# Graph attention, layer 1: the turn of two sets' gathered rows, as 16 row tiles of 64 keys in one place instead of 8 full transposes in two

## The chip, the cores and the metric

The kernel runs on one core of a Trainium2 chip. Its time is device microseconds (us) of one execution. TensorE is called PE in the profile (PEld is its weight load), VectorE is DVE, ScalarE is ACT, GpSimd is POOL, SyncE is SP.

## The reference

A two-layer graph attention over 2048 nodes in 8 batches with a residual and two layer norms. All data is float32; `adj` is a 0/1 matrix that all batches and heads share.

```python
def _gat_layer(h, mask, b):
    scores = jnp.einsum('...nd,...md->...nm', h, h)
    scores = jnp.where(mask, scores, NEG)
    attn = jax.nn.softmax(scores, axis=-1)
    return jnp.einsum('...nm,...md->...nd', attn, h) + b

mask = graph + jnp.eye(N, dtype=graph.dtype) > 0            # N = 2048
h = jnp.einsum('bnc,hdc->bhnd', x, Wh)                      # 8 batches, 4 heads, 64 wide
out_h = _gat_layer(h, mask[None, None], bh[None, :, None, :])        # layer 1
z = jax.nn.leaky_relu(cat, negative_slope=0.2)              # cat: the heads side by side
h2 = jnp.einsum('bnk,dk->bnd', z, Wo)
out2 = _gat_layer(h2, mask[None], bo)                       # layer 2
...                                                         # leaky, norm, residual, norm
```

## The kernel before

The graph is sparse except for 56 hub nodes, which are done densely. The other 1992 nodes stand in 166 sets of 12. For each set the kernel finds a list of at most 128 keys (the neighbours of any of its nodes), gathers the 128 rows of these keys from a table in device memory (an indirect DMA of POOL, L829), and does the attention of the set's nodes against them. One gathered row holds a node in all 8 batches: four pairs of batches (`q`), each of 130 numbers, of which 128 are the 64 channels of two batches (`p`), between two columns of ones.

Layer 1 is a loop over 83 groups of two sets. The order of the work is the order in which the loop is written; each engine runs its own instructions in that order and waits on counts of the others. The loop is a software pipeline: step i works at several groups at once. On TensorE one step does, in this order:

- `scores` of group i+1 (L858): the turned rows as weights, 64x64 tiles of the array, four at a time;
- `project` of group i-1 (L551), 64x64 tiles, from the tile `otb` that ACT copies in `keep_values` (L907) out of the turned values;
- `values` of group i (L883): the exponentials `e` as weights, 128x64 tiles, two at a time;
- `second_maps` of group i-2 (L917), 128x64 tiles, and `second_rows` of group i-3 (L927, a transpose), both into the tile `cat`;
- `columns` for group i+4 (L843, full 128x128), also into `cat`: the products from which the scores' moving side `y` is made;
- `turn(bank[0], ...)`: four transposes of 128x128 (L532), the rows of the first set of group i+3 into one PSUM bank;
- `turn_values` of group i (L900): four transposes of the weighted values `osb` that DVE has divided (L890, L891);
- `turn(bank[1], ...)`: four more transposes, the rows of the second set.

A float32 matmul stands in the trace as two records of its form, a transpose as one.

The other engines in a step: ACT adds the bias to `project`'s result (`z`, L538, two instructions), then copies the two banks with the turned rows of group i+2 to the tile `xTg` in SBUF (L1182, two copies), raises `e` to its exponential (L870), copies the columns (`keep_columns`, `y<-cat`, L849) and the turned values (`keep_values`, `otb<-o`, L907). DVE subtracts the mask from the scores (`weigh`, L863), divides the values (L890, L891), does the leaky maximum of `z` (L543), copies the second maps out of `cat` (`keep_own`, `own<-cat`, L922), adds the bias to the second rows (`keep_rows`, `rowt<-cat`, L931), and then does one or two jobs of the search for the key lists, while there are any. The banks `bank[0]` and `bank[1]` are single: what turns rows into them has to wait until ACT has copied the rows of the group before.

Of the kernel before, what the change touches and what calls it, by code (L numbers as in the profile page):

```python
# [359 lines left out]
def fast_kernel(ctx: ExitStack, tc: tile.TileContext, x, adj, Wh, bh, Wo, bo, gamma, beta, out, flag):  # L360


    nc = tc.nc
    B, N, C = x.shape
    H, D, _ = Wh.shape
    P = 128
    NB = N // P
    Q = B // 2
# [6 lines left out]
    NG = NS // 2  # L375
    M = SET * H
# [23 lines left out]
    def half(k):  # L400
        return slice(k * 64, (k + 1) * 64)

    def rows_tile(name):
        return rowp.tile([P, Q, PW], F32, tag="rows", name=name)
# [7 lines left out]
    ident = const.tile([P, P], F32, name="ident")  # L412
# [116 lines left out]
    def turn(tp, rows):  # L529

        for q in range(Q):
            nc.tensor.transpose(tp[:, q * P:(q + 1) * P], rows[:, q, 1:1 + P], ident)  # L532

    def leaky(cat, n, name):

        z = work.tile([P, HP, 2, n], F32, tag="z", name=name, bufs=3)
        for hp in range(HP):
            nc.scalar.activation(z[:, hp], cat[:, :, hp * n:(hp + 1) * n], AF.Identity, bias=bhp[:, hp:hp + 1], scale=1.0)  # L538
        return z

    def leak(z):
        f = z.rearrange("p q s n -> p (q s n)")
        nc.vector.scalar_tensor_tensor(f, f, SLOPE, f, OP.mult, OP.max)  # L543

    def project(ot, cat, n):

        for hp in range(HP):
            for s in range(2):
                for j in range(2):
                    h = 2 * hp + j  # L550
                    nc.tensor.matmul(cat[half(j), s, hp * n:(hp + 1) * n], whT[half(s), h * D:(h + 1) * D],  # L551
                                     ot[half(s), h, :], start=True, stop=True)
# [268 lines left out]
    rows = {}  # L821
    held = {}
# [9 lines left out]
    def own_rows(m):  # L832
# [3 lines left out]
        src = xT[:, :, HUB:].rearrange("c q (k s) -> c s q k", s=NS)[:, 4 * m:4 * m + w]  # L836
        nc.gpsimd.tensor_copy(t[:, :w * 48].rearrange("c (s q k) -> c s q k", s=w, q=Q), src)

    def columns(g, cat):

        n = min(4, NS - 4 * (g // 2)) * 48
        for k in range(2):
            nc.tensor.matmul(cat[:, k, 2 * GM:2 * GM + n], gram[:, g % 2 * 2 + k, :], held["x", g // 2][:, :n], start=True, stop=True)  # L843
# [5 lines left out]
        nc.scalar.copy(held["y", g // 2][:, :n, g % 2 * 2:g % 2 * 2 + 2], cat[:, :, 2 * GM:2 * GM + n].rearrange("p a n -> p n a"))  # L849

    def scores(g, sp):
        xt = held.pop(("T", 1, g)).rearrange("c j (q n) -> c j q n", q=Q)
        y = held["y", g // 2][:, g % 2 * GM:(g % 2 + 1) * GM, :].rearrange("p n h -> p (n h)")
        for j in range(2):
            for q in range(Q):
                for p in range(2):
                    for r in range(2):
                        nc.tensor.matmul(sp[half(r), p, (q * 2 + j) * M:(q * 2 + j + 1) * M], xt[half(p), j, q, half(r)],  # L858
                                         y[half(p), (j * Q + q) * M:(j * Q + q + 1) * M], start=True, stop=True)

    def weigh(g, sp):
        e = es[g % 2]
        nc.vector.tensor_tensor(e[:, :16 * M].rearrange("p (a q n) -> p a q n", a=2, q=Q),  # L863
                                sp[:, :, :8 * M].rearrange("p a (q n) -> p a q n", q=Q),
                                mask[:, 2 * g:2 * g + 2, :].rearrange("p s n -> p (s n)").unsqueeze(1).unsqueeze(1)
                                .to_broadcast([P, 2, Q, 2 * M]), OP.subtract)

    def lift(g):
        e = es[g % 2]
        nc.scalar.activation(e[:, :16 * M], e[:, :16 * M], AF.Exp, bias=shifts[:, 0:1], scale=1.0)  # L870
# [3 lines left out]
    def values(g, op):  # L874
        e = es[g % 2]
        rw = [rows.pop((1, 2 * g + j)) for j in range(2)]
        for q in range(Q):
            for j in range(2):
                for p in range(2):
                    c0 = (p * 8 + q * 2 + j) * M  # L880
                    o0 = q // 2 * OQ + q % 2 * (D + 2) + p

                    nc.tensor.matmul(op[half(p), j, o0:o0 + K1], e[:, c0:c0 + 64], rw[j][:, q, sums(p)], start=True, stop=True)  # L883

    def invert(g, op):
        v = op.rearrange("a j (k c) -> a (j k) c", k=2)[:, :, :2 * (D + 2)].rearrange("a w (s c) -> a w s c", s=2)
        osb = held["o", g] = work.tile([P, 4, 2, D], F32, tag="osb", name=f"osb{g}")
        r = rall[:, g, :].rearrange("a (w s) -> a w s", w=4)
        for p in range(2):
            nc.vector.reciprocal(r[half(p)], v[half(p), :, :, p * K1])  # L890
        nc.vector.tensor_tensor(osb, v[:, :, :, 1:K1], r.unsqueeze(3).to_broadcast([P, 4, 2, D]), OP.mult)  # L891
# [34 lines left out]
    def second_rows(g, pr):  # L926
        nc.tensor.transpose(pr, held.pop(("own", g)), ident)  # L927
# [135 lines left out]
    bank = [psumk.tile([P, 512], F32, name=f"bank{k}") for k in range(2)]  # L1063
# [3 lines left out]
    def one(name, tag):  # L1067
        return psum1.tile([P, 2, 512], F32, tag=tag, name=name)
# [94 lines left out]
    for i in range(-3, NG + 3):  # L1163
        if 0 <= i + 1 < NG:
            sp = one(f"s{i + 1}", "S")
            scores(i + 1, sp)
            weigh(i + 1, sp)
        if i >= 1 and slow and len(slow) % 3:
            slow.pop(0)()
        cat = one(f"cat{i}", "C") if i <= NG else None  # L1170
        if i < NG:
            ph, pr = cat[:, 0, 384:384 + GM], cat[:GM, 1, 384:512]
        else:
            cat = one(f"cat{i}", "S" if i == NG + 1 else "C")
            ph, pr = cat[:, 0, :GM], cat[:GM, 1, :P]
        if 0 <= i - 1 < NG:
            project(held.pop(("ot", i - 1)), cat, GM)
            held["z", i - 1] = leaky(cat, GM, f"z{i - 1}")
        if 0 <= i + 2 < NG:
            t = held["T", 1, i + 2] = work.tile([P, 2, 512], F32, tag="xTg", name=f"xTg{i + 2}", bufs=3)  # L1180
            for k in range(2):
                nc.scalar.copy(t[:, k, :], bank[k])  # L1182
        if 0 <= i + 1 < NG:
            lift(i + 1)
        if 0 <= i < NG:
            op = one(f"o{i}", "O")
            values(i, op)
            invert(i, op)
        if 0 <= i + LOOK < NG and i > -3:
            for j in range(2):  # L1190
                gather(table1, 2 * (i + LOOK) + j, 1, rows_tile)
        if NG - LOOK <= i < NG - 1:
            for j in range(2):
                k = 2 * (i - NG + LOOK) + j
                hub_block(k, rows_tile(f"gh{k}"))
        if i + 6 < NG and i % 2 == 0 and i >= -2:
            own_rows((i + 6) // 2)
        if i >= 60 and i % 2 == 0 and ahead_of_second:
            ahead_of_second.pop(0)()
        if 0 <= (i - 30) // 2 <= NV:  # L1200
            (add_beta if i % 2 else load_own)((i - 30) // 2)
        if 0 <= i - 1 < NG:
            leak(held["z", i - 1])
        if i >= 0:
            if turns():
                some(1)
            if slow and len(slow) % 3 == 0:
                slow.pop(0)()
            more(1)
            if todo3 and i == todo3[0][0]:  # L1210
                r = todo3.pop(0)[1:]
                make_keys(*r, late_two)
                if r == (1, 1):
                    picks += pick(1)
                    done = 2 * FIRST
            if not picks:
                ready = done
            if not picks and not todo3 and done < NS:
                picks = pick(2)
                done = NS  # L1220
            assert i + 1 + LOOK >= NG or 2 * (i + 1 + LOOK) + 1 < ready

        if 0 <= i - 2 < NG:
            second_maps(i - 2, ph)
        if 0 <= i - 3 < NG:
            second_rows(i - 3, pr)
        if 2 <= i + 4 < NG + NG % 2:
            columns(i + 4, cat)
        if 0 <= i - 2 < NG:
            keep_own(i - 2, ph)  # L1230
        if 0 <= i - 3 < NG:
            keep_rows(i - 3, pr)
        for _ in range((2 if i < 22 or i % 2 else 1) if i >= 0 else 0):
            if not turns():
                some(1)
        if 2 <= i + 4 < NG + NG % 2:
            keep_columns(i + 4, cat)
        if 0 <= i + 3 < NG:
            turn(bank[0], rows[1, 2 * (i + 3)])
        if 0 <= i < NG:  # L1240
            turn_values(i, op)
            keep_values(i, op)
        if 0 <= i + 3 < NG:
            turn(bank[1], rows[1, 2 * (i + 3) + 1])
        if NG - 3 <= i < NG:
            hub_step(i - NG + 3, bank[0])
    for k in range(3, 9):
# [300 lines left out]
```

## Time and profile before

| what | value |
|---|---|
| three runs | 861.07, 863.03, 866.28 us, median 863.03 |
| the profiled execution | 860.43 us, of which the core's span is 858.6 us |
| PE busy / weight load busy | 760.2 us (89%) / 651.4 us (76%) |
| DVE, ACT, POOL busy | 601.5 us (70%), 537.9 us (63%), 485.3 us (57%) |
| granted TensorE clock, mean of the span | 0.97 |
| steps of layer 1: first and last start of `values` | 136.79 us and 577.75 us (83 steps) |

A busy PE is not PE at its peak, since records of matmuls that follow each other overlap. So the time of a run of matmuls is read from where one run starts to where the next one starts, and the step from one start of `values` (L883) to the next. The stretch before 136 us makes the lists and the hubs, the stretch after 583 us is layer 2; the change leaves both alone.

### The profile page before, as it was taken

What the parts mean: (1) busy time and instruction counts of PE and PEld (TensorE: products, weight loads), DVE (VectorE), ACT (ScalarE), POOL (GpSimd) and SP (SyncE); (2) the same over time, 40 slices, a digit from 0 to 9 for tenths busy, and PEclk for the clock granted to TensorE, in tenths of its full rate; (3) what the DMA queues carried; (4) which work ended last, traced back from release to release, by engine and by line L of the source; (5) the groups of instructions that cost most, each with busy time, mean ns of one, the idle gap of its engine ahead of it and who ended that gap; (6) DMA issues with size and microseconds to landing.
All of it is one profiled execution on the core that took longest, in us unless ns stands there. A gap on an engine that the chain in (4) does not pass through costs nothing.

```text
span 858.6 us, 42821 instructions
## 1 busy us (share of the span) xinstructions
PE 760.2 (89%) x18461; PEld 651.4 (76%) x18461; DVE 601.5 (70%) x1368; ACT 537.9 (63%) x1175; POOL 485.3 (57%) x619
## 2 busy tenths in 40 slices
PE   4798788899999999999999999998999899998940
PEld 3575567788888898988998988887887778876730
DVE  4347974688887788886556665564248999997895
ACT  2354545566666666666666666663558889887741
POOL 5444563564454456655665666504777777777700
PEclk9899989999999999999999999999999999999975
DMA  6999652443333344444444444335975666665621
GB/s 124 214 243 268 192 171 53 111 118 89 92 88 89 83 118 134 129 120 129 128 130 120 123 123 117 90 108 146 310 202 170 181 189 193 191 180 166 185 55 34
DMA packets 81791, 122.53 MB, mean 143 GB/s; under 512 B 35568, under 2 KB 51852, under 8 KB 81594
## 3 DMA queue, kind: packets, MB, share of 16 engines
q0 software_dynamic: 26784, 65.84, 28.7%
q1 hardware_dynamic: 50374, 52.71, 21.5%
q8 instruction: 148, 2.42, 1.2%
q10 hardware_dynamic: 4436, 1.15, 0.7%
q14 instruction: 49, 0.40, 0.2%
HBM read 123.91 MB, written 18.48 MB: 166 GB/s over the span
## 4 chain that ended last, share of the span: by engine, by line
PE 61%; DVE 17%; DMA 9%; issue 5%; SPq 3%; ACT 3%; POOL 2%; DVEq 0%; POOLq 0%; ACTq 0%
PE o L883 10%; PE s L858 9%; PE bank L532 8%; PE cat L843 6%; DMA rows<-table,index 5%; PE cat L551 4%; PE o L900 3%; PE cat L917 3%; PE t L532 3%; SPq L1400 3%; PE oh L639 3%; PE cat L927 2%; PE sh L621 2%; DMA out_dram<-y_s 2%; PE o L1317 2%
## 5 line engine op out<-in xcount | busy, mean ns | idle before, releaser
L829 POOL DMA_INDIRECT g<-table,index x166 | 175.6, 1058 | 173.6 <-PE o L883 144.8
L829 POOL DMA_INDIRECT rows<-table,index x166 | 173.7, 1046 | 55.1 <-issue 23.2
L863 DVE TENSOR_TENSOR e<-s,mask 128x768 f32<-128x768 f32 x83 | 79.3, 955 | 73.5 <-PE s L858 70.3
L538 ACT ACTIVATE z<-cat,bhp 128x192 f32<-128x192 f32 x166 | 60.7, 416 | 79.4 <-PE cat L551 79.3
L532 PE MATMUL t<-ident,rows 128*128 128x128 f32 x664 | 93.0, 279 | 11.2 <-DMA rows<-table,index 5.2
L883 PE MATMUL o<-g,e 128*64 128x65 f32 x2656 | 97.9, 225 | 3.9 <-issue 3.8
L532 PE MATMUL bank<-ident,g 128*128 128x128 f32 x664 | 99.5, 273 | 1.4 <-DVE e L1059 1.2
L883 PEld LDWEIGHTS o<-g,e 128*64 128x64 f32 x2656 | 85.4, 138 | 14.6 <-issue 4.8
L858 PEld LDWEIGHTS s<-y,xTg 64*64 64x64 f32 x5312 | 85.2, 135 | 13.8 <-issue 13.8
L858 PE MATMUL s<-y,xTg 64*64 64x48 f32 x5312 | 95.5, 221 | 0.0
L1436 ACT COPY xts<-t 128x512 f32<-128x512 f32 x166 | 88.7, 583 | 8.6 <-PE t L532 7.7
L532 PEld LDWEIGHTS t<-ident,rows 128*128 128x128 f32 x664 | 72.9, 141 | 24.0 <-issue 12.2
L1182 ACT COPY xTg<-bank 128x512 f32<-128x512 f32 x166 | 89.0, 596 | 2.5 <-PE bank L532 2.5
L532 PEld LDWEIGHTS bank<-ident,g 128*128 128x128 f32 x664 | 79.0, 141 | 4.1 <-issue 1.3
L849 ACT COPY y<-cat 128x384 f32<-128x384 f32 (+1 forms) x82 | 41.6, 508 | 64.1 <-PE o L900 34.5
L870 ACT ACTIVATE e<-e,shifts 128x768 f32<-128x768 f32 x83 | 80.1, 965 | 2.0 <-DVE e L863 2.0
L711 POOL TENSOR_SCALAR a<-raw 120x1024 bf16<-120x1024 int32 (+1 forms) x34 | 38.5, 1134 | 65.5 <-DMA raw<-in_adj_dram 50.6
L628 ACT ACTIVATE e<-e,shifts 128x896 f32<-128x896 f32 x32 | 33.4, 1043 | 58.1 <-DVE e L625 47.8
L890 DVE RECIPROCAL rall<-o 64x8 f32<-64x8 f32 x166 | 33.9, 205 | 47.8 <-PE o L883 46.5
L843 PE MATMUL cat<-xo,gram 128*128 128x192 f32 (+1 forms) x328 | 66.6, 326 | 0.0
L891 DVE TENSOR_TENSOR osb<-o,rall 128x512 f32<-128x512 f32 x83 | 57.4, 692 | 2.9
L625 DVE TENSOR_TENSOR e<-sh,maskh 128x896 f32<-128x896 f32 x32 | 34.8, 1087 | 31.6 <-PE sh L621 26.6
(195 smaller groups left out, 1529.8 us busy)
## 6 DMA issues: line engine op xcount, KB each, us to landing
raw<-in_adj_dram SPq DMA_DIRECT2D x32, 480.0 KB
table<-xb SPq DMA_DIRECT2D x22, 256.0 KB
xr_s<-table SPq DMA_DIRECT2D x21, 256.0 KB
table<-x SPq DMA_DIRECT2D x16, 260.0 KB
table<-rowt SPq DMA_DIRECT2D x164, 24.4 KB
xb<-in_x_dram SPq DMA_DIRECT2D x164, 24.0 KB
out_dram<-y_s SPq DMA_DIRECT2D x162, 24.0 KB
x<-in_x_dram SPq DMA_DIRECT2D x24, 128.0 KB
```

The source lines that it names most:

```text
L532: nc.tensor.transpose(tp[:, q * P:(q + 1) * P], rows[:, q, 1:1 + P], ident)
L538: nc.scalar.activation(z[:, hp], cat[:, :, hp * n:(hp + 1) * n], AF.Identity, bias=bhp[:, hp:hp + 1], scale=1.0)
L829: nc.gpsimd.indirect_dma_start(out=t.rearrange("n q c -> n (q c)"), out_offset=None, in_=table, in_offset=bass.IndirectOffsetOnAxis(ap=ind ...
L843: nc.tensor.matmul(cat[:, k, 2 * GM:2 * GM + n], gram[:, g % 2 * 2 + k, :], held["x", g // 2][:, :n], start=True, stop=True)
L849: nc.scalar.copy(held["y", g // 2][:, :n, g % 2 * 2:g % 2 * 2 + 2], cat[:, :, 2 * GM:2 * GM + n].rearrange("p a n -> p n a"))
L858: nc.tensor.matmul(sp[half(r), p, (q * 2 + j) * M:(q * 2 + j + 1) * M], xt[half(p), j, q, half(r)], y[half(p), (j * Q + q) * M:(j * Q + q ...
L863: nc.vector.tensor_tensor(e[:, :16 * M].rearrange("p (a q n) -> p a q n", a=2, q=Q), sp[:, :, :8 * M].rearrange("p a (q n) -> p a q n", q= ...
L870: nc.scalar.activation(e[:, :16 * M], e[:, :16 * M], AF.Exp, bias=shifts[:, 0:1], scale=1.0)
L883: nc.tensor.matmul(op[half(p), j, o0:o0 + K1], e[:, c0:c0 + 64], rw[j][:, q, sums(p)], start=True, stop=True)
L891: nc.vector.tensor_tensor(osb, v[:, :, :, 1:K1], r.unsqueeze(3).to_broadcast([P, 4, 2, D]), OP.mult)
L1182: nc.scalar.copy(t[:, k, :], bank[k])
L1436: nc.scalar.copy(xts[s // 2 % 4][:, s % 2, :], tp)
```

## The change

The two calls of `turn` are taken out of the loop. In their place a new function turns the rows of both sets of group i+3 in one run, between `second_rows` and `columns`. It takes each 128 keys as two halves of 64: half 0 is a transpose on the upper 64 rows of the array and goes to `bank[0]`, half 1 one on the lower 64 rows and goes to `bank[1]`. So there are 16 transposes, with 64x128 weights (the rows) and a 64x64 identity that moves, where there were 8 with 128x128 and a 128x128 identity; each bank now holds one half of the keys of both sets, and `scores` reads its weights by the new layout. `turn_values` now comes right after `columns`, and `scores` right after `turn_values`.

```diff
+    def turn_rows(g):
+
+        for j in range(2):
+            rw = rows[1, 2 * g + j]
+            for q in range(Q):
+                for r in range(2):
+                    c0 = (j * Q + q) * 64
+                    nc.tensor.transpose(bank[r][:, c0:c0 + 64], rw[half(r), q, 1:1 + P], ident[half(r), half(r)])
+
...
     def scores(g, sp):
-        xt = held.pop(("T", 1, g)).rearrange("c j (q n) -> c j q n", q=Q)
+        xt = held.pop(("T", 1, g)).rearrange("c r (j q n) -> c r j q n", j=2, q=Q)
...
-                        nc.tensor.matmul(..., xt[half(p), j, q, half(r)],
+                        nc.tensor.matmul(..., xt[half(p), r, j, q, :],
...
+        if 0 <= i + 3 < NG:
+            turn_rows(i + 3)
         if 2 <= i + 4 < NG + NG % 2:
             columns(i + 4, cat)
...
-        if 0 <= i + 3 < NG:
-            turn(bank[0], rows[1, 2 * (i + 3)])
         if 0 <= i < NG:
             turn_values(i, op)
             keep_values(i, op)
-        if 0 <= i + 3 < NG:
-            turn(bank[1], rows[1, 2 * (i + 3) + 1])
```

Lines from the new function on stand 9 further down in the changed kernel: `scores` is L867, `values` L892, `second_maps` L926, `second_rows` L936, `turn_values` L909, `keep_own` L931, `keep_rows` L940, `keep_columns` L858, `keep_values` L916, the copies of the banks L1191. The new transposes are L846, `columns` is L852. `project` and ACT's `z` keep L551 and L538.

TensorE's instructions of one step before, from `second_maps` to the next `scores`, with what they wait for in brackets (`g` is a gathered tile; the counts are those of ACT, DVE, PE itself and the gathers, DMASW):

```order
L917 MATMUL cat_3228<-z_3103,woT 64x2x4x12 x3
L927 MATMUL cat_3228<-ident,own_3167 96x128
L843 MATMUL cat_3228<-xo_2910,gram 128x192 x2
L532 MATMUL bank_1747<-ident,g_28_3017 128x128 [waits DMASW1_49,Activation_49]
L532 MATMUL bank_1747<-ident,g_28_3017 128x128 x3
L900 MATMUL o_3244<-ident,osb_3261 128x112 [waits DVE_49]
L900 MATMUL o_3244<-ident,osb_3261 128x112 x3
L532 MATMUL bank_1748<-ident,g_29_3021 128x128 [waits DMASW2_49,Activation_49]
L532 MATMUL bank_1748<-ident,g_29_3021 128x128 x3
L858 MATMUL s_3307<-y_2929,xTg_3240 64x48 [waits PE_49]
```

The bank copies of ACT are waited for at the first transpose into each bank; here `columns` stand ahead of the first of them. The same place of a step in the changed kernel (bank_1747 is `bank[0]`, bank_1748 is `bank[1]`; the transposes go on in turn where rows are left out):

```order
L926 MATMUL cat_2832<-z_2718,woT 64x2x4x12 x3
L936 MATMUL cat_2832<-ident,own_2780 96x128
L846 MATMUL bank_1747<-ident,g_20_2616 128x64 [waits DMASW1_49,Activation_49]
L846 MATMUL bank_1748<-ident,g_20_2616 128x64 [waits Activation_49]
...
L846 MATMUL bank_1747<-ident,g_21_2620 128x64 [waits DMASW2_49]
L846 MATMUL bank_1748<-ident,g_21_2620 128x64
...
L852 MATMUL cat_2832<-xo_2497,gram 128x192 x2
L909 MATMUL o_2848<-ident,osb_2865 128x112 [waits DVE_49]
L909 MATMUL o_2848<-ident,osb_2865 128x112 x3
L867 MATMUL s_2919<-y_2536,xTg_2844 64x48 [waits PE_49]
```

Both waits for ACT's copies have moved ahead of `columns`, into the first two transposes. DVE's row in a step of the changed kernel, which reads as it did before but for the line numbers:

```order
L899 RECIPROCAL rall<-o_7726 64x8 [waits PE_49]
L899 RECIPROCAL rall<-o_7726 64x8
L900 TENSOR_TENSOR osb_7743<-o_7726,rall 128x512 [waits DVE_49]
L543 SCALAR_TENSOR_TENSOR z_7719<-z_7719 128x384 [waits Activation_49]
L931 COPY own_7789<-cat_7710 128x96 [waits PE_49,Pool_49]
L940 TENSOR_TENSOR rowt_115<-cat_7710,bob 96x128 [waits DMAHW7_49,DMAHW0_49]
L872 TENSOR_TENSOR e_110<-s_7804,mask 128x768 [waits PE_49]
```

Nothing moved on DVE, but what L931 waits for did: TensorE's count is raised once for `second_maps`, `second_rows` and `columns` together, at the last matmul of `columns`, before and after; with the change that one raise covers the 16 transposes too, which stand ahead of it. ACT's row is unchanged as well:

```order
L538 ACTIVATE z_8460<-cat_8451,bhp 128x192 [waits PE_49]
L538 ACTIVATE z_8460<-cat_8451,bhp 128x192
L1191 COPY xTg_8463<-bank_1747 128x512
L1191 COPY xTg_8463<-bank_1748 128x512
L879 ACTIVATE e_111<-e_111,shifts 128x768 [waits DVE_49,Activation_49]
L858 COPY y_8536<-cat_8451 128x192x2 [waits DVE_49,PE_49]
L916 COPY otb_8542<-o_8467 128x4x48 [waits PE_49,Activation_49]
```

Here too only the source of the waits moved: L858's wait for DVE is one for `keep_rows` (both read `cat`), and `keep_values` stands behind it.

More of the change, by code (lines that the diff above doesn't have):

```diff
@@ L857, in scores @@
                     for r in range(2):
-                        nc.tensor.matmul(sp[half(r), p, (q * 2 + j) * M:(q * 2 + j + 1) * M], xt[half(p), j, q, half(r)],
+                        nc.tensor.matmul(sp[half(r), p, (q * 2 + j) * M:(q * 2 + j + 1) * M], xt[half(p), r, j, q, :],
                                          y[half(p), (j * Q + q) * M:(j * Q + q + 1) * M], start=True, stop=True)
```

## The prediction

> **What bounds the kernel now.** I read the chain that ended last first, then the engines' shares by stage, then one quiet step of layer 1 engine by engine. The chain (shares of the span) and the waits of TensorE inside layer 1 (engine, line, what ended the wait: us in total, times, longest):
>
> ```profile
> PE 61%; DVE 17%; DMA 9%; issue 5%; SPq 3%; ACT 3%; POOL 2%; DVEq 0%; POOLq 0%; ACTq 0%
> 176.00:550.00 374.00, 364.10 (x9749) 327.94 (x9748) 268.05 (x698) 247.28 (x570) 217.14 (x276) 1.00 0.41 112
> PE o L883 <- issue: 3.8, 7, 0.9
> PE cat L551 <- ACT otb L907: 3.3, 5, 1.3
> PE cat L917 <- issue: 0.9, 2, 0.6
> ```
>
> From 176 to 550 us TensorE is busy 364 of 374 us (the second row's first pair; DVE 268, ACT 247) and waits little. Next a quiet step on TensorE (start, us, line, operation, count), from one start of `values` to the next:
>
> ```profile
> 410.72 1.15 PE L883 MATMUL o<-g,e 128*64 128x65 f32 x32
> 411.71 0.50 PE L917 MATMUL cat<-z,woT 128*64 128x96 f32 x8
> 412.14 0.31 PE L927 MATMUL cat<-ident,own 128*96 128x128 f32 x1
> 412.29 0.82 PE L843 MATMUL cat<-xo,gram 128*128 128x192 f32 x4
> 412.94 0.60 PE L532 MATMUL bank<-ident,g 128*128 128x128 f32 x4
> 413.38 0.55 PE L900 MATMUL o<-ident,osb 112*128 112x112 f32 x4
> 413.76 0.60 PE L532 MATMUL bank<-ident,g 128*128 128x128 f32 x4
> 414.30 1.15 PE L858 MATMUL s<-y,xTg 64*64 64x48 f32 x64
> 415.27 0.53 PE L551 MATMUL cat<-otb,whT 64*64 64x96 f32 x16
> 415.72 0.45 PE L883 MATMUL o<-g,e 128*64 128x65 f32 x8
> ```
>
> The step is 5.00 us, without a hole: TensorE's own row of work sets it. The whole layer runs from
>
> ```profile
> 136.79 1.15 PE L883 MATMUL o<-g,e 128*64 128x65 f32 x32
> ...
> 577.75 0.92 PE L883 MATMUL o<-g,e 128*64 128x65 f32 x24
> ```
>
> that is 441 us for 82 spacings; by the starts of these groups 51 of them lie within 0.02 us of 5.00, the rest are longer by waits (a few at the end are shorter). But behind TensorE another chain is close. The same step on ACT and DVE, and a later step in which `project` (L551) did wait for it:
>
> ```profile
> 410.86 0.73 ACT L538 ACTIVATE z<-cat,bhp 128x192 f32<-128x192 f32 x2 [0.94 <-PE cat L551]
> 411.48 1.07 ACT L1182 COPY xTg<-bank 128x512 f32<-128x512 f32 x2
> 413.99 0.51 ACT L849 COPY y<-cat 128x384 f32<-128x384 f32 x1 [0.60 <-DVE rowt L931]
> 414.38 0.55 ACT L907 COPY otb<-o 128x192 f32<-128x192 f32 x2
> ...
> 412.99 0.55 DVE L543 SCALAR_TENSOR_TENSOR z<-z 128x384 f32<-128x384 f32 x1
> 413.45 0.25 DVE L922 COPY own<-cat 128x96 f32<-128x96 f32 x1
> 413.62 0.28 DVE L931 TENSOR_TENSOR rowt<-cat,bob 96x128 f32<-96x128 f32 x1
> ...
> 477.02 0.55 ACT L907 COPY otb<-o 128x192 f32<-128x192 f32 x2
> 477.62 0.56 PE L551 MATMUL cat<-otb,whT 64*64 64x96 f32 x16
> 478.11 0.28 PE L883 MATMUL o<-g,e 128*64 128x65 f32 x2
> ...
> L922 DVE COPY own<-cat 128x96 f32<-128x96 f32 x71 | 17.8, 251 | 3.8 <-PE cat L843 3.8
> ```
>
> `own` follows the leaky maximum, `rowt` follows `own`, `y` waits for `rowt`, `otb` follows `y` and ends at 414.93, and `project` needs `otb`: it starts at 415.27, so 0.29 us are spare beyond the 0.05 us from ACT's end (477.57) to PE's start (477.62). The last row says what `own` itself waits for when DVE is idle: the end of `columns` (L843). Here they end at 413.11, ahead of the leaky maximum, and cost nothing.
>
> **The change, part by part.** I count from the start of `values`, V.
>
> *The eight transposes go.* They hold TensorE 413.38 - 412.94 = 0.44 and 414.30 - 413.76 = 0.54 us. That the second run is 0.10 us longer, with the same work, is my price of a change of tile shape: 64x64 tiles follow it, while the first is followed by more transposes. The same surplus stands at L551 to L883 and L917 to L927, so it is paid when only the rows or only the columns of the tile change. The first load after it is not covered either: L927 takes 0.15 where a transpose in a row takes 0.11 (0.44 / 4), so 0.04 us for a fast load; and `columns` right behind 128x64 tiles took 0.75 us to the next start instead of 0.65:
>
> ```profile
> 155.15 0.92 PE L843 MATMUL cat<-xo,gram 128*128 128x192 f32 x4
> 155.90 0.60 PE L532 MATMUL bank<-ident,g 128*128 128x128 f32 x4
> ```
>
> *The sixteen row tiles come.* No row shows a transpose on 64x128 tiles. Lower bound: two halves run side by side as the 64x64 tiles of L858 do, 64 records in 0.97 us, so (0.97 - 0.04) / 16 = 0.058 us for one wave; 8 waves of two are 0.46 us. Upper bound: one after another, 16 x 0.058 = 0.93. I take 0.46: L858's tiles overlap on both halves of the rows, and the load of 128 columns fits, since transpose loads are short (mean ns after the bar):
>
> ```profile
> L927 PEld LDWEIGHTS cat<-ident,own 128*96 128x96 f32 x80 | 9.9, 124 | 9.4
> L793 PEld LDWEIGHTS bank<-ident,share 128*128 128x128 f32 x2 | 0.3, 138 | 0.8 <-ACT xTg L1182 0.8
> L1123 PEld LDWEIGHTS bank<-share,own 128*120 128x120 f32 x8 | 0.9, 186 | 0.0
> L1123 PEld LDWEIGHTS bank<-share,ownh 128*56 128x56 f32 x8 | 0.8, 129 | 0.1
> ```
>
> 96 to 128 columns cost 14 ns in a transpose (0.44 ns a column, 56 ns for 128), but 56 to 120 columns cost 57 ns in a plain matmul (0.89 a column).
>
> The Trainium skill (TensorE: Matmul & The Clock Gate, LDWEIGHTS) says a load takes its columns divided by 1.2 ns, whatever the rows: 107 ns for 128 columns, so halving the keys would halve nothing. The plain loads here agree with it, the transposes' do not; what a wave would then cost is the second rival.
>
> *TensorE's own sum.* From L927 to the next L858 it was 414.30 - 412.14 = 2.16 us. Now: L927 0.15 and a change of shape 0.10; row tiles 0.04 + 0.46 and a change 0.10; `columns` 0.75; `turn_values` 0.39 (413.76 - 413.38) and the change 0.10. That is 2.09 us: a gain of only 0.07 us a step, the two new changes of shape eat the rest of it.
>
> *The wait that moves.* The row tiles need both banks, and ACT's copies end at 411.48 + 1.07 = 412.55, V + 1.83; with 0.05 the second row tile starts at V + 1.88. TensorE is there at 1.42 + 0.25 = 1.67 (L927's start and what follows it), so it waits 0.21 us. Before, `columns` stood between and covered this. Queued behind this wait are `columns`, `turn_values`, `scores`.
>
> *The chain that takes over.* Row tiles V + 1.88 + 0.04 + 0.46 + 0.10 = 2.48. `columns` end 0.82 + 0.10 later, 3.40 (V + 2.39 before). Only then does `own` get its count: 0.09 for the hand-over (as from rowt's end, 413.90, to y's start, 413.99) gives 3.49. rowt starts 0.17 after own and takes 0.28: 3.94. y after 0.09: 4.03. From y's start to otb's end 0.94: 4.97. `project` after 0.05: 5.02; TensorE itself would have been there at about 4.66 (2.48 + 0.75 + 0.49 + 0.97 = 4.69). After a wait, `project` to `values` takes 478.11 - 477.62 = 0.49: the next V is at 5.51. A quiet step becomes 5.5 us, +0.51.
>
> *Edits at nothing.* Copies, sizes and order on ACT, DVE, POOL are unchanged; `scores`' new weight layout reads 64 columns in a row as before. DVE's list jobs after rowt (under 2 us) now start 0.5 us later in a step that is 0.5 us longer. The gathers are issued two steps before their use, so turning them 0.7 us earlier in the step is covered; without that cover each us late is a us of wait.
>
> *Sum.* 51 quiet steps x 0.51 = 26 us. Nine steps with TensorE late inside `values` or `second_maps` (the two "issue" rows) hide 0.21 of it: 9 x 0.30 = 2.7. The other 22, in which ACT or DVE extra work already sets the chain, or which have no row turn at the end, between 0 and 0.51 each; I take 0.2: 4.4. Together 33 us: 860.43 + 33 = 893.5 us against the profiled execution; the median of the runs is 2.6 us above that, so 896 us.
>
> **Rivals.**
> 1. *Cheap exit from the row tiles*: 128 columns stay 128 columns, so the drain and the open load (0.10 + 0.10) vanish. Speaks for it: no row has this very change; against: L551 to L883 changes rows alone and pays. Step 5.31: 51 x 0.31 + 9 x 0.10 + 22 x 0.1 = 19 us, 882 us.
> 2. *No overlap*: the change does not do what it says. If halves follow each other, 0.46 us more a step; if loads go at the plain rate, waves of 0.109 us (a full transpose now), 0.41 more. Then the step is 5.9 to 6.0 and the sum 62 to 69 us: 925 to 932 us. Against it: L858's waves.
> 3. *Faster*: TensorE's sum stays the bound. Then 0.07 us x 51 is 4 us less, 859 us; with free changes of shape the spare 0.29 us a step would be all that can be had, 15 us, 848. It decides if `columns` end by V + 2.89 (3.40 - 0.51); they take 0.82 and the copies end at 1.83, so the row tiles would need under 0.2 us, or must not have to wait for the copies. The built order says that they do.
> 4. *Nothing to see*: gain and wait cancel within 0.5%, about what a measurement tells from no change; same condition as 3.
>
> **Chances.** My forecast 0.64 (its own range 884 to 908, from the hand-overs of 0.05 to 0.1 us and the 22 mixed steps); rival 1 0.13; rival 2 0.16 (half of it each way); rival 3 0.03; rival 4 0.04. Slower by over 0.5% then 0.93. The range leaves out rivals 2, 3 and 4 and reaches over rival 1: 874 to 918 us.
>
> **What would show it.** Right: quiet steps of about 5.5 us from L892 to L892; L846 starting its second record just after the second xTg copy; 8 waves of about 58 ns; L931 starting just after L852's end; waits of `project` (L551) on otb (L916) in nearly every step, some 0.3 us. Wrong: pairs of L846 at 110 ns (rival 2), L852 following L846 without the surplus (rival 1), or own starting right behind the leaky maximum, which would break the chain and with it the sign.

## The result, and the profile after

| | kernel before | changed kernel |
|---|---|---|
| median of four runs each | 864.65 us | 900.88 us (899.14 to 904.0) |
| the profiled execution, its span | 860.43 us, 858.6 us | 899.60 us, 897.8 us |
| layer 1, first to last start of `values` | 441.0 us | 477.1 us |

The changed kernel is slower: ratio 1.0446, interval 1.0408 to 1.0484. Of the 39.2 us between the two profiled executions 36.1 lie in layer 1, 2.4 ahead of it and 0.6 behind it. The first and the last start of `values` in the changed kernel (timeline of TensorE):

```profile
139.22 1.15 PE L892 MATMUL o<-g,e 128*64 128x65 f32 x32
...
616.33 1.15 PE L892 MATMUL o<-g,e 128*64 128x65 f32 x32
```

The chain that ended last, by engine (page of the changed kernel), the busy times from 176 to 550 us (its length, then PE, PEld, DVE, ACT, POOL, the granted clock, the DMA share, GB/s), and three waits of the whole run (engine, what it does, what ended the wait: us in total, times, longest):

```profile
PE 52%; DVE 18%; issue 8%; DMA 8%; ACT 8%; SPq 4%; POOL 1%; DVEq 0%; ACTq 0%; POOLq 0%
```

```profile
176.00:550.00 374.00, 357.66 (x9543) 302.83 (x9541) 253.41 (x658) 228.71 (x525) 198.63 (x254) 1.00 0.38 104
```

```profile
ACT y L858 <- DVE rowt L940: 114.2, 76, 3.2
DVE own L931 <- PE cat L852: 54.5, 72, 2.5
PE cat L551 <- ACT otb L916: 16.6, 72, 1.2
```

TensorE's share of the chain fell from 61 to 52% and ACT's rose from 3 to 8%: the chain now leaves TensorE in most steps. `own` waits for the end of `columns` 72 times (3.8 us in all before, 54.5 now), and `project` waits for `otb` 72 times, 16.6 us, where it had waited 5 times, 3.3 us. TensorE is still busy for 358 of 374 us in the middle of the layer. That share says nothing about the loss, since a run that stretches over a wait counts as busy: the row tiles' run below contains one.

A quiet step of the changed kernel on TensorE, ACT and DVE (start, us, engine, line, operation, count, in brackets the idle time ahead and what ended it):

```profile
437.59 1.15 PE L892 MATMUL o<-g,e 128*64 128x65 f32 x32
...
439.01 0.31 PE L936 MATMUL cat<-ident,own 128*96 128x128 f32 x1
439.25 0.93 PE L846 MATMUL bank<-ident,g 64*128 64x64 f32 x16
440.11 0.92 PE L852 MATMUL cat<-xo,gram 128*128 128x192 f32 x4
440.86 0.55 PE L909 MATMUL o<-ident,osb 112*128 112x112 f32 x4
441.34 1.15 PE L867 MATMUL s<-y,xTg 64*64 64x48 f32 x64
442.67 0.56 PE L551 MATMUL cat<-otb,whT 64*64 64x96 f32 x16 [0.18 <-ACT otb L916]
443.16 0.34 PE L892 MATMUL o<-g,e 128*64 128x65 f32 x4
...
438.35 1.07 ACT L1191 COPY xTg<-bank 128x512 f32<-128x512 f32 x2
441.68 0.52 ACT L858 COPY y<-cat 128x384 f32<-128x384 f32 x1 [1.42 <-DVE rowt L940]
442.07 0.55 ACT L916 COPY otb<-o 128x192 f32<-128x192 f32 x2
...
441.13 0.26 DVE L931 COPY own<-cat 128x96 f32<-128x96 f32 x1 [0.73 <-PE cat L852]
441.31 0.28 DVE L940 TENSOR_TENSOR rowt<-cat,bob 96x128 f32<-96x128 f32 x1
```

The step is 443.16 - 437.59 = 5.57 us; 60 of the 82 spacings lie within 0.025 us of 5.575. `columns` end at 441.03, V + 3.44; `own` starts behind them, where before it started behind the leaky maximum of `z` (V + 2.73). From `own`'s start to the next `values` it is 443.16 - 441.13 = 2.03 us: rowt, y, otb and `project` in a row.

### The profile page after: what moved, and what is told of

It reads as the page before. It is cut to its first block, busy times and chain, and to the rows that moved or that the text cites. A ratio compares the mean times of both kernels' runs of the same rounds, so it can differ in the third digit from the quotient of the medians.

```text
span 897.8 us, 44068 instructions
## 1 busy us (share of the span) xinstructions
PE 785.0 (87%) x19125; PEld 649.6 (72%) x19125; DVE 603.8 (67%) x1368; ACT 538.3 (60%) x1175; POOL 484.0 (54%) x619
## 4 chain that ended last, share of the span: by engine, by line
PE 52%; DVE 18%; issue 8%; DMA 8%; ACT 8%; SPq 4%; POOL 1%; DVEq 0%; ACTq 0%; POOLq 0%
PE o L892 9%; PE bank L846 7%; PE cat L852 7%; PE cat L551 5%; ACT otb L916 4%; PE t L532 3%; DMA rows<-table,index 3%; PE oh L639 3%; PE cat L926 3%; SPq L1407 2%; DVE rowt L940 2%; PE sh L621 2%; PE bank L1294 2%; PE cat L936 2%; PE o L1324 2%
## 5 line engine op out<-in xcount | busy, mean ns | idle before, releaser
L858 ACT COPY y<-cat 128x384 f32<-128x384 f32 (+1 forms) x82 | 42.1, 514 | 119.9 <-DVE rowt L940 114.2
L538 ACT ACTIVATE z<-cat,bhp 128x192 f32<-128x192 f32 x166 | 60.7, 416 | 61.4 <-PE cat L551 61.3
L892 PE MATMUL o<-g,e 128*64 128x65 f32 x2656 | 96.5, 226 | 0.0
L867 PE MATMUL s<-y,xTg 64*64 64x48 f32 x5312 | 95.7, 221 | 0.0
L867 PEld LDWEIGHTS s<-y,xTg 64*64 64x64 f32 x5312 | 85.5, 135 | 12.1 <-issue 0.8
L892 PEld LDWEIGHTS o<-g,e 128*64 128x64 f32 x2656 | 84.9, 139 | 9.9 <-issue 0.2
L1191 ACT COPY xTg<-bank 128x512 f32<-128x512 f32 x166 | 89.0, 596 | 2.5 <-PE bank L846 2.5
L846 PE MATMUL bank<-ident,g 64*128 64x64 f32 x1328 | 76.0, 233 | 4.9 <-ACT otbh L664 1.4
L852 PE MATMUL cat<-xo,gram 128*128 128x192 f32 (+1 forms) x328 | 74.6, 350 | 0.0
L846 PEld LDWEIGHTS bank<-ident,g 64*128 64x128 f32 x1328 | 58.0, 139 | 22.2 <-ACT otbh L664 1.8
L551 PE MATMUL cat<-otb,whT 64*64 64x96 f32 x1328 | 46.9, 256 | 18.7 <-ACT otb L916 16.6
```

Source lines behind the costliest of these rows:

```text
L846: nc.tensor.transpose(bank[r][:, c0:c0 + 64], rw[half(r), q, 1:1 + P], ident[half(r), half(r)])
```

## The experiments

My theory: the place costs the time. `own` is let go only by the count that TensorE raises behind `columns`, and `columns` now stand behind the row tiles, which wait for the bank copies. The rival: the shape costs it, sixteen small transposes and two more changes of tile shape.

The experiments ran on chips (0, 2, 5 and 6 in the record) on which the kernel before takes 1009 to 1021 us, not 865; so each is held only against runs of the kernel before on the same chip. The chip of the first measurement, here "the first chip", has no number in the record, so that the chip itself makes this difference is not shown.

**Both kernels once more.** No edit.

> The kernel before once more, as it is, for its trace on such a chip. Theory: TensorE alone sets the step here too, with its 274 instructions at the slower pace seen in the other runs (17 to 19 ns each), 5.0 to 5.3 us; own follows the leaky maximum as on the first chip. Rival: own or otb set the step already, with project waiting for otb in most steps.

> The changed kernel once more, as it is, for its time and its trace on a chip where the kernel before takes 1010 us. Theory (place: the wait for the copies and own's count): the ratio is about what it was, 1.03 to 1.07; if TensorE's count for the columns comes 0.75 us after their last record here, as it did with the copies first, the step is about 6.2 us. Rival (the cost of the change is TensorE's work): with TensorE slower, the step follows its instructions, 290 a step where there were 274, 6% more than before.

Measured: the kernel before 0.9998 [0.9953, 1.0042] of itself, the changed kernel 1073.52 us against 1011.58, 1.0646 [1.057, 1.0722]. The median of 44 steps (the 16th to the 59th) is 5.41 us before and 6.26 after, so something on these chips adds to both. Most of what it adds lies elsewhere: of the 152 us by which the span of the kernel before is longer here than on the first chip, 23.5 lie in layer 1 (464.5 us for 441.0, at a granted clock of 0.99 for 1.00) and 118 behind it. What the change adds still lies in layer 1, 56.1 of the 58.3 us between these two traces. A step of each, the kernel before first (TensorE and ACT, then TensorE and DVE):

```profile
327.52 0.31 PE L927 MATMUL cat<-ident,own 128*96 128x128 f32 x1
328.76 0.55 PE L900 MATMUL o<-ident,osb 112*128 112x112 f32 x4
329.67 1.51 PE L858 MATMUL s<-y,xTg 64*64 64x48 f32 x64
...
330.42 0.54 ACT L907 COPY otb<-o 128x192 f32<-128x192 f32 x2 [0.55 <-PE o L900]
```

```profile
355.81 0.92 PE L852 MATMUL cat<-xo,gram 128*128 128x192 f32 x4
357.04 1.23 PE L867 MATMUL s<-y,xTg 64*64 64x48 f32 x64
...
359.55 0.45 PE L892 MATMUL o<-g,e 128*64 128x65 f32 x8
...
357.53 0.26 DVE L931 COPY own<-cat 128x96 f32<-128x96 f32 x1 [1.43 <-PE o L909]
```

Before: the turned values end at 329.31, but `otb`, which waits for them, starts at 330.42. After: `columns` end at 356.73, but `own`, which waits for them, starts at 357.53, and the profile names L909 as the releaser, the next run on TensorE. In both, the count of a finished run becomes visible some 0.8 to 1.1 us late, when TensorE is well into `scores`; from the end of `columns` to `own`'s start the median of the 44 steps of the changed kernel is 0.78 us here and 0.11 on the first chip. The lateness is there before DVE: in the trace's own list of TensorE's counts, the one for `columns` is raised at 357.44, 0.71 us behind their last record, and `own` starts 0.09 us after it. From `own` on the chain is the one of the first chip: 359.55 - 357.53 = 2.02 us. So the theory's chain is there, with a later start, as expected for the changed kernel. For the kernel before the expectation missed: its step is 5.41 and not 5.0 to 5.3 us, and `project` starts within 0.1 us of the end of `otb` in 35 of 44 steps (in 2 on the first chip), as the rival had it. `scores` are stretched there too, 1.19 us from their first record to their last where it was 0.93.

**The row tiles behind the columns.** The new transposes stay, in another place:

```diff
-        if 0 <= i + 3 < NG:
-            turn_rows(i + 3)
         if 2 <= i + 4 < NG + NG % 2:
             columns(i + 4, cat)
...
             keep_columns(i + 4, cat)
+        if 0 <= i + 3 < NG:
+            turn_rows(i + 3)
```

> The 16 row tiles stay as they are, but stand behind the columns (and their copy) instead of ahead of them. Theory (place: the wait for the bank copies and the count that own waits for): the copies end at V + 1.83 and the columns are over by V + 2.3, so no wait; own's count comes at the end of the columns again, V + 2.4, so own follows the leaky maximum as before. TensorE's own sum sets the step: L936 0.15, columns 0.65 + 0.10, row tiles 0.63, turned values 0.39 + 0.04 + 0.10 = 2.06 us where it was 2.16 before the change, step 4.90 us, 5 to 8 us less than before the change in all: about 857. Rival (the row tiles and their changes of shape are what costs): the step stays near 5.5 us, near 895 to 900.

> Once more the row tiles behind the columns. Where the kernel before takes about 863 us: step 4.95 to 5.0, about 857 us. Where it takes about 1010 us: 1.005 of it, as the first run of this kernel. The rival that the shape of the tiles costs time: 1.02 or more on either.

Measured: 1.0051 [1.0022, 1.008], and 1.0025 [0.9996, 1.0054] in the second comparison. The rival, 1.02 or more, falls: the sixteen row tiles with their two changes of shape cost nothing to speak of where they don't stand ahead of `columns`. This kernel has as many TensorE instructions a step as the changed one, so their number alone, the rival of the changed kernel's second run, falls with it. TensorE, DVE and ACT in a step of the second run:

```profile
313.66 0.31 PE L936 MATMUL cat<-ident,own 128*96 128x128 f32 x1
...
314.55 0.71 PE L846 MATMUL bank<-ident,g 64*128 64x64 f32 x16
315.73 1.56 PE L867 MATMUL s<-y,xTg 64*64 64x48 f32 x64
...
314.98 0.25 DVE L931 COPY own<-cat 128x96 f32<-128x96 f32 x1
...
316.53 0.54 ACT L916 COPY otb<-o 128x192 f32<-128x192 f32 x2 [0.51 <-PE o L909]
```

`own` is back at V + 2.74 (V is 312.24). L936 to L867 is 315.73 - 313.66 = 2.07 us, against 329.67 - 327.52 = 2.15 in the kernel before on such a chip: the small gain of TensorE's sum that I had forecast (0.07) is there in this order. It buys nothing here: `project` starts right behind `otb` and its late count, and `scores` take 1.35 us from first to last record (median). The step of 4.90 us expected for the first chip was not tested.

**The old transposes in the new place.** In the kernel before, both runs of full transposes are moved ahead of `columns`; no row tiles:

```diff
+        if 0 <= i + 3 < NG:
+            turn(bank[0], rows[1, 2 * (i + 3)])
+            turn(bank[1], rows[1, 2 * (i + 3) + 1])
         if 2 <= i + 4 < NG + NG % 2:
             columns(i + 4, cat)
...
-        if 0 <= i + 3 < NG:
-            turn(bank[0], rows[1, 2 * (i + 3)])
...
-        if 0 <= i + 3 < NG:
-            turn(bank[1], rows[1, 2 * (i + 3) + 1])
```

> The kernel before with its eight full 128x128 transposes, all in one run between the row turn and the columns: the new place with the old shape. Theory (place): no wait for the copies (the second bank's first transpose comes at V + 2.0, its copy ends at 1.83), but 0.87 us of transposes stand ahead of the columns; these end at V + 3.26, own starts at 3.36, rowt ends at 3.82, otb at 4.85, the step is 5.40 us, in all about 888 us. Rival (shape): TensorE's work and shapes are those of before, so the step stays 5.00 us and the time 863.

Measured: 1.0314 [1.0253, 1.0375]. The place alone makes the kernel slower, with no row tile in it. This trace also shows both kinds of step side by side (TensorE and DVE, two steps, the late one first):

```profile
361.20 0.82 PE L843 MATMUL cat<-xo,gram 128*128 128x192 f32 x4
...
364.95 1.15 PE L883 MATMUL o<-g,e 128*64 128x65 f32 x32
...
367.39 0.82 PE L843 MATMUL cat<-xo,gram 128*128 128x192 f32 x4
...
370.43 0.39 PE L883 MATMUL o<-g,e 128*64 128x65 f32 x5
...
362.94 0.26 DVE L922 COPY own<-cat 128x96 f32<-128x96 f32 x1 [1.37 <-PE o L900]
368.41 0.26 DVE L922 COPY own<-cat 128x96 f32<-128x96 f32 x1 [0.64 <-PE cat L843]
```

`columns` end at 362.02 and at 368.21 (V + 3.26 in the second step). In the first step the count reaches DVE 0.92 us later, in the second 0.20, and from `own` to the next `values` both take the same: 364.95 - 362.94 = 2.01 and 370.43 - 368.41 = 2.02. Of the 44 steps `own` starts within 0.44 us of the end of `columns` in 31 (median step 5.50) and 0.92 us or more behind it in 13 (6.38). So once `own` is bound by the end of `columns`, the time of a step is the arrival of that count plus 2.0 us, with the old shape of the transposes as with the new one. The changed kernel, whose `columns` end 0.18 us later, is late in nearly all its steps (42 of 44), and the other half of its 6.5% on these chips goes with that. The later end of `columns` is not the reason: with both edits (below) they end at V + 3.22, earlier than here, and their count is raised over 0.5 us late in 38 of 44 steps, against 13 here. So the row tiles ahead of `columns` may themselves make the count late on these chips; that rival was not tested, and why the count is late was not found.

**`own` not behind the columns.** In the changed kernel the second maps and rows go into the tile of the scores instead of `cat`, so that their count is their own:

```diff
-            ph, pr = cat[:, 0, 384:384 + GM], cat[:GM, 1, 384:512]
+            at = sp if 15 <= i < NG - 1 else cat
+            ph, pr = at[:, 0, 384:384 + GM], at[:GM, 1, 384:512]
```

> The changed kernel, but from step 15 on second_maps and second_rows write into free columns of the scores' tile instead of the tile of the columns, so that own and rowt no longer wait for the columns, nor y for rowt. Theory (the chain over own takes over): project no longer waits for otb (ready at V + 4.5, TensorE there at 4.7); the step is TensorE's row of work with its wait of 0.22 for the copies, 5.18 us instead of 5.575, so 65 steps x 0.39 = 26 us less than the changed kernel: about 875. Rival (row tiles and the wait for the copies are all there is to it): the step stays 5.57, 900 us.

> second_maps and second_rows in the scores' tile from step 15 on, once more, for the same reason. Theory: y follows the columns' end by 0.1, otb is ready at V + 4.5, TensorE comes to project at 4.7 without a wait, step 5.18 us, about 875. Rival 1 (own and rowt are not on the chain): 5.57 us, 900. Rival 2 (the late count belongs to this kernel): 5.7 to 6.0 us, above 900.

Measured: 1.0404 [1.035, 1.0457] and 1.0355 [1.0297, 1.0412]. `own` is on time again, but the step came down from 6.26 to only 5.7 us. DVE and ACT in a step of the second run:

```profile
332.72 0.25 DVE L931 COPY own<-s 128x96 f32<-128x96 f32 x1
332.89 0.28 DVE L940 TENSOR_TENSOR rowt<-s,bob 96x128 f32<-96x128 f32 x1
...
334.15 0.51 ACT L858 COPY y<-cat 128x384 f32<-128x384 f32 x1 [1.49 <-PE o L909]
```

`own` starts at V + 2.73 and `rowt` ends at V + 3.18, but `y` starts at V + 4.16: it copies the columns themselves and waits for their count. My estimate of the whole loss as `own`'s wait was too simple for these chips: cutting one reader off saves 0.5 us a step, the other reader of the same late count stays. The second run was meant for a chip like the first, but the kernel before took 1009 us there too. So neither its forecast of 875 us nor its second rival, that the late count belongs to this kernel, was put to the test.

**The copies first.** In the changed kernel ACT copies the banks ahead of the bias of `project`'s result (the block with `project` and `leaky` moves behind the copies `xTg<-bank`), so that the row tiles need not wait:

```diff
-        if 0 <= i - 1 < NG:
-            project(held.pop(("ot", i - 1)), cat, GM)
-            held["z", i - 1] = leaky(cat, GM, f"z{i - 1}")
...
+        if 0 <= i - 1 < NG:
+            project(held.pop(("ot", i - 1)), cat, GM)
+            held["z", i - 1] = leaky(cat, GM, f"z{i - 1}")
```

> The changed kernel, but ACT copies the two banks ahead of project's bias (z) instead of behind it, so the copies end at about V + 0.55 and the row tiles do not wait for them. Theory: the 0.22 us of wait leave the chain, the rest of it stays (columns end at V + 3.21, otb at 4.80): step 5.35 us, about 16 us less than the changed kernel: 884. Rival 1 (chain over own is not what sets the step): with no wait TensorE's sum gives 4.95 us and about 860. Rival 2 (the wait is covered by the later one of project): no change, 900.

> The copies ahead of project's bias, once more, on a chip where the kernel before takes what it took at first. The first run of it fell on a chip on which the kernel before takes 1011 us and on which TensorE's count for the columns came 0.75 us after their last record. Theory: columns end 0.22 us earlier in the step, V + 3.21, own follows them by 0.11, otb ends at 4.80, step 5.35 us instead of 5.575, about 884 us. Rival 1 (the chain over own does not set the step): TensorE's own sum, 4.95 us, about 860. Rival 2 (the late count belongs to this kernel and not to the chip): step 6.2 us as on the other chip, about 930.

Measured: 1.0632 [1.0576, 1.0687] and 1.0656 [1.06, 1.0713], no gain over the changed kernel. Two causes show in the rows (second run, TensorE, then ACT):

```profile
341.25 1.15 PE L892 MATMUL o<-g,e 128*64 128x65 f32 x32
342.36 0.55 PE L926 MATMUL cat<-z,woT 128*64 128x96 f32 x8
...
343.09 0.71 PE L846 MATMUL bank<-ident,g 64*128 64x64 f32 x16
343.73 0.92 PE L852 MATMUL cat<-xo,gram 128*128 128x192 f32 x4
...
341.53 0.78 ACT L538 ACTIVATE z<-cat,bhp 128x192 f32<-128x192 f32 x2
```

The row tiles now take 343.73 - 343.09 = 0.64 us, without the wait of 0.22. But `z`, which reads `cat`, ends at 342.31, and the second maps, which write `cat`, start only then: V + 1.11 instead of 0.98. So `columns` end just 0.04 us earlier; and the count behind them is as late as before. The second run came out at its rival 2, but on a chip where the kernel before is slow as well, so it does not tell what the edit is worth on the first chip.

**Both edits together.**

> The changed kernel with both changes of the earlier runs: the second maps and rows in a tile that the columns do not share, and the copies of the banks ahead of the bias of project's result on ACT. Where the kernel before takes about 863 us: the wait for the copies (0.2) and the wait for own (0.3) both go, step about 4.95, 857 to 862 us. Where it takes about 1010 us: the copies gave nothing there and the other tile took 0.53 us off the step, so step 5.73 and 1.035 to 1.04 of the kernel before. The rival that the copies gave nothing only because own hid it: step 5.5, 1.02.

Measured: 1.0366 [1.0314, 1.0419], as expected for these chips and the same as with `own` freed alone; the rival's 1.02 falls. With the maps in the other tile the second maps don't wait for `z`, and the gain reaches `columns`, but not `y` (TensorE, then ACT):

```profile
340.04 1.15 PE L892 MATMUL o<-g,e 128*64 128x65 f32 x32
...
341.46 0.31 PE L936 MATMUL s<-ident,own 128*96 128x128 f32 x1
341.70 0.70 PE L846 MATMUL bank<-ident,g 64*128 64x64 f32 x16
342.34 0.92 PE L852 MATMUL cat<-xo,gram 128*128 128x192 f32 x4
...
343.57 0.44 PE L867 MATMUL s<-y,xTg 64*64 64x48 f32 x15
344.32 1.00 PE L867 MATMUL s<-y,xTg 64*64 64x48 f32 x49 [0.31 <-issue]
...
344.45 0.52 ACT L858 COPY y<-cat 128x384 f32<-128x384 f32 x1 [2.52 <-PE o L909]
```

`columns` end at V + 3.22, 0.22 earlier than in the changed kernel, and `y` starts at V + 4.41, just after TensorE resumes from a stop of 0.31 us inside `scores` for which the profile names no cause. On these chips the wait for the copies is thus worth nothing; what it is worth on the first chip was not measured.

**The halves apart.** All eight transposes of the upper half first, then the eight of the lower half:

```diff
-        for j in range(2):
+        for r, j in ((0, 0), (0, 1), (1, 0), (1, 1)):
...
-                for r in range(2):
```

> The changed kernel, but the 16 row tiles in another order: all eight on the upper 64 rows of the array first, then all eight on the lower ones, instead of in turn. Theory (the pairs run side by side): without pairs the run takes 16 x 0.058 + 0.04 + 0.10 = 1.07 us from its first record to the columns, and it need not wait for the second copy (its first record for bank[1] comes at V + 2.2); the columns end at V + 3.65 instead of 3.44, and the step is 0.2 us longer than the changed kernel's, 5.8 us, or 6.4 to 6.5 where the kernel before takes 1010 us. Rival (the array does one tile at a time anyway, or the load of 128 columns sets the pace): the records follow each other at the pace that they have in the changed kernel, 0.03 us each, and the run is no longer than there.

Measured: 1.0654 [1.0589, 1.072], with a step of 6.31 us where 6.4 to 6.5 were expected. Its lines are one lower (TensorE):

```profile
343.09 1.00 PE L845 MATMUL bank<-ident,g 64*128 64x64 f32 x16
344.02 0.92 PE L851 MATMUL cat<-xo,gram 128*128 128x192 f32 x4
```

Sixteen tiles with the halves in turn take 0.64 us when nothing is waited for (the two sections above), and 344.02 - 343.09 = 0.93 one half after the other. So the pairs overlap, which was rival 2's question in the prediction, and 0.04 + 0.46 + 0.10 = 0.60 was nearly right. The run is shorter than the 1.07 us expected here because the second half begins before the first has ended: where one half runs alone, the records stand 61 to 62 ns apart, but in each of the 44 steps three pairs in the middle start within 10 ns of each other. Each half of the array also writes a bank of its own, so these runs don't tell whether two halves or two banks make the overlap possible. One half after the other needs the second bank only after some tiles of the first half, so nothing waits for the copies, but the lost overlap (0.29) is more than that wait (0.22).

**The row tiles behind the turned values**, next to `scores`, so that there is one change of shape less:

```diff
-        if 0 <= i + 3 < NG:
-            turn_rows(i + 3)
...
+        if 0 <= i + 3 < NG:
+            turn_rows(i + 3)
```

> The row tiles as they are, but behind the turned values, just ahead of the scores: columns, turned values, row tiles. Theory (place): no wait for the copies, own behind the leaky maximum, and one change of shape less, since the columns and the turned values follow the row turn in its own shape; the turned values wait 0.19 us for osb. TensorE: 0.15 + 0.65 + 0.19 + 0.39 + 0.10 + 0.63 = 2.11 us from the row turn to the scores where it was 2.16: step 4.95 us, 859 us; where the kernel before takes 1010 us, and project waits for otb since the count for the turned values comes late, that count comes 0.5 us earlier, so the step falls from 5.4 to 5.0 or 5.2, 980 to 1000 us. Rival (the count is as late as the scores' run makes it, whatever stands ahead): 5.4 us and the time of the kernel before, within 1%.

Measured: 1.0066 [1.0031, 1.01] against 1.0654 for the halves apart on the same chip: again no row tiles ahead of `columns`, and the loss is gone. The time is the rival's, but not for the rival's reason. A step on TensorE, then ACT:

```profile
332.65 0.44 PE L867 MATMUL s<-y,xTg 64*64 64x48 f32 x14
333.43 1.07 PE L867 MATMUL s<-y,xTg 64*64 64x48 f32 x50 [0.34 <-issue]
334.29 0.54 PE L551 MATMUL cat<-otb,whT 64*64 64x96 f32 x14
...
333.53 0.54 ACT L916 COPY otb<-o 128x192 f32<-128x192 f32 x2 [0.54 <-PE o L909]
```

`otb` ends at 334.07, 0.22 us ahead of `project`, and in the median of the 44 steps 0.64 us ahead: the count for the turned values comes earlier, as the theory had it. The step is 5.47 us all the same, because `scores` take 1.33 us from their first record to their last (0.93 on the first chip). In 40 of the 44 steps they hold a stop of over 0.2 us from one record to the next, for which the profile names no cause. So on these chips a step without row tiles ahead of `columns` is not held by `otb` alone.

## Why the prediction was right, point by point

- *The chain that takes over* held link by link on the first chip (forecast against measured, from V): `columns` end 3.40 / 3.44, `own` 3.49 / 3.54, rowt ends 3.94 / 4.00, y 4.03 / 4.09, otb ends 4.97 / 5.03, `project` 5.02 / 5.08, next V 5.51 / 5.57.
- *The wait that moves*: 0.21 forecast; the second row tile started 0.22 us after the first, at V + 1.88 as forecast. Where the copies were early (the copies first, both edits), the run lost 0.22 us.
- *The sixteen row tiles*: 0.60 with load and exit; 0.63 from the second tile, and 0.64 in the runs without a wait, in pairs that follow each other after 57 to 59 ns (forecast 58), after a first one of 109. The Trainium skill (TensorE: Matmul & The Clock Gate, LDWEIGHTS) gives a load its columns divided by 1.2 ns, 107 ns for 128 columns. Here sixteen transposes with such loads fit into 0.93 us with the halves apart, 61 to 62 ns from one to the next where one half runs alone; for transposes the measurement decides against the page. That was rival 2 in its second form.
- *The change of shape*: L852 to L909 is 440.86 - 440.11 = 0.75 us, forecast 0.75. Rival 1, a free exit, fell with it.
- *TensorE's own sum*: 2.16 to 2.09 forecast, a gain of 0.07 us a step. In the order of the change, with both edits and no wait, it is 343.57 - 341.46 = 2.11 us, a gain of 0.05; with the tiles behind `columns` it is 2.07 for 2.15. (TensorE's arrival at `project`, which the prediction gives as about 4.66, is 4.69 by its own terms; nothing hangs on it.) Rivals 3 and 4 needed this sum to stay the bound, and it did not.
- *The sum*: 51 quiet steps were to cost 26 us and took 31.9 (0.58 in a typical one, more in a few: the 5th went from 5.00 to 7.13); the other 31 were to cost 7.1 and took 4.3, since ten of them got no longer: the new step covers the waits that had made them long (6.21 became 5.57). Layer 1 came to 36.1 for 33, closer than its parts, as the two misses have opposite signs. The 2.4 us ahead of the layer I had put at nothing.
- *A term that I had only for one chip*: 0.09 us from the end of `columns` to `own`. On the first chip it was 0.11, on the others 0.78, and with it the same change cost 6.5% instead of 4.5.

What carries the sign, that the order and not the shape of the transposes makes the kernel slower, is shown by the tiles behind `columns` and by the old transposes ahead of them, on the other chips; on the first chip only the two kernels themselves ran, and there it rests on the chain of the trace. Of the size on the other chips, the place alone, with the old transposes, accounts for 3.1%, with 13 late steps of 44 in it; the rest goes with the late counts, in which the row tiles may have a part.

## What to carry to other kernels

Before a run of matmuls is moved on TensorE, list who waits for the runs that it then stands ahead of: a consumer on DVE or ACT is let go by the count behind the last run that it needs, and a reader of a shared PSUM tile may need a later run than its own data. A row of work that is 0.05 us shorter loses when it puts 0.9 us ahead of the start of a chain with 0.3 us to spare. Where one run needs two buffers freed, turning through them in pairs overlaps but asks for both buffers at once (0.22 us of waiting for 0.29 of overlap here).

## What the runs showed that I had not expected

The same kernel takes 865 us on one chip and 1009 to 1021 on others, with the clock nearly the same (mean 0.97, against 0.944 in a run of 1011.2 us). Most of the difference lies behind layer 1 and was not looked into. In layer 1 it goes with counts of TensorE that reach DVE and ACT 0.7 to 1.1 us after the run that they stand for, and not always: in one trace 31 steps were on time and 13 late. In the changed kernel's trace the count for `columns` is over 0.5 us late in 41 of the 44 steps, and in all of these it arrives 0.31 to 0.62 us after TensorE has begun the long run of 64 small matmuls of `scores`. In some versions a stop of over 0.2 us inside `scores` without a named cause goes with late counts (40 of 44 steps with the tiles behind `columns`), in others hardly (2 of 44 in the changed kernel). That TensorE's handling of instructions is slower on those chips would fit, but no run here tests it. A kernel whose other engines follow TensorE closely is hurt by this more than one with slack: the changed kernel lost 6.5% there, and two versions that let `own` go early lost 0.3 to 0.7%. No version was faster than the kernel before.
